# Pairing the state tiles of a selective scan: u*B, the states and h*C in one SBUF tile, on one Trainium2 core

## The chip, the cores and the metric

The kernel runs on one core of a Trainium2 chip. The metric is the device time of one execution in microseconds (us), the median of several runs. The core's engines are named as in the profile: PE (TensorE), DVE (VectorE), ACT (ScalarE), POOL (GpSimd) and SP (SyncE, which issues the DMAs of the main loop). SBUF is the on-chip memory that all of them reach; PSUM is the smaller memory that the matmuls write to.

## The reference

The input is x, 32 x 96 x 56 x 56, in float32. A ConvNeXt block (7x7 depthwise convolution, layer norm, a 96-384-96 GELU network, residual) is followed by two Mamba layers over the 3136 pixels of each image as a sequence, a fusing 1x1 convolution with a pooled branch, a batch norm and a residual. Nearly all of the time goes to the two Mamba layers:

```
xs, z  = split(layernorm(seq) @ in_w)           # 192 channels each
xc     = silu(conv4(xs) + conv_b)
dt, Bm, Cm = split(xc @ xproj_w)                # 6, 16, 16
delta  = softplus(dt @ dt_w + dt_b)
h[t]   = exp(delta[t] * A) * h[t-1] + delta[t] * Bm[t] * xc[t]   # 192 channels x 16 states
y      = sum over states of h * Cm + Dp * xc
seq    = seq + (y * silu(z)) @ out_w
```

With u = delta * xc, the work of the recurrence for each channel and state is: e = exp(delta*A), the product u*B, the scan h = e*h + u*B, the product h*C, and a sum of h*C over the 16 states.

## The kernel before

A sequence of 3136 is cut into 4 chunks of CH = 784 tokens. A **stage** is one chunk of one image in one layer, so there are 32 x 4 x 2 = 256 stages. The 192 channels are six blocks j of 32 channels; with 4 of the 16 states on the partitions beside the 32 channels, one block has NG = 4 groups g. So a stage has 24 **steps** n, one scan of 128 x 784 each. The block's copy of delta (`d4`) and the copies of B and C (`bc`) are spread over the partitions by DMAs from DRAM that SP issues.

The order of each engine's instructions is written out by hand (`manual_schedule`). The final loop goes through the steps; at each it issues the exps of one or two steps ahead (`exps`), the carry of the state (`keep_state`), the scan (`scan`), and the sum over states of three or four steps back (`add_up`). Everything else (projections, norms, the ConvNeXt block and the convolution of later images, DMAs) consists of small pieces, each with a slot number that says after which step of which stage it is issued. Each engine then runs its own list in order and waits on semaphores.

In step (j, g) of the kernel before:

- ACT writes e = exp(A*d4) (L890). For the four blocks j = 0, 1, 3, 4 and g = 0, 1, 2 it goes into an SBUF tile `da`; for g = 3, and for the blocks in `POOLED` (2 and 5), into a PSUM slot `w`.
- u*B: for j = 0, 1, 3, 4, PE spreads u over the partitions into a PSUM slot `u4` (`spread`, L905) and DVE multiplies by B (`times_b`, L878). The product for g = 0, 1, 2 goes to PSUM (`w`, or `u4` in place), and for g = 3 to an SBUF tile `da`. For the `POOLED` blocks POOL multiplies in SBUF (`pooled`, L915, into a `da`).
- DVE scans (L938, TENSOR_TENSOR_SCAN), from e and u*B into slot g of `ring`, a tile of four states called h in the profile. One of the scan's two tensors is always in PSUM and the other in SBUF:

```
e = wide(g % 2)[:, 0:CH] if in_psum(j, g) else product_tile(S, j, g)
db = da if in_psum(j, g) else S.u4[:, 0:CH] if g == 2 else S.w
```

- POOL multiplies h by C into `da` (L942), one instruction of 128x784 for each step.
- PE adds the four states of each channel up with a 0/1 matrix `ssum` (L975), two matmuls of 32 columns for each step. When two blocks are done, DVE multiplies the sum by silu(z) (`gate`, L956).

`keep_state` (L949) copies the last column of h for the next chunk of the image. `product` (L712) is u = delta*xc on POOL, in two instructions.

Of the kernel before, what the change touches and what calls it, by code (L numbers as in the profile page):

```python
# [37 lines left out]
ALU = mybir.AluOpType  # L38
# [23 lines left out]
def convnext_mamba_kernel(  # L62
# [211 lines left out]
    for i in range(2):  # L274
        d = {}
        lg, lb = column(ln_g[i], C, f"lg{i}"), column(ln_b[i], C, f"lb{i}")
        wz = const.tile([C + 1, 2 * DIN], F32, name=f"inw{i}", tag=f"inw{i}")
        norm_weights(wz, in_w[i], lg, lb)
        wx = const.tile([C + 1, 4, DIN], F32, name=f"wx{i}", tag=f"wx{i}")
        nc.gpsimd.dma_start(wx, taps[i].partition_broadcast(C + 1))  # L280
        for k in range(4):
            nc.vector.tensor_tensor(wx[:, k, :], wx[:, k, :], wz[:, 0:DIN], ALU.mult)
        d["wx"], d["wz"] = wx, wz[:, DIN : 2 * DIN]
# [60 lines left out]
    with ExitStack() as main:  # L344
# [7 lines left out]
        def work(shape, name, bufs):  # L352

            pool, n = (pre[0], 3) if pre else (wp, bufs)
            return pool.tile(shape, F32, name=name, tag=name, bufs=n)
# [42 lines left out]
        xins = {}  # L398

        def block0(b, c, s):  # L400
# [16 lines left out]
            def load_x():  # L417
                if s == 0:
                    xins[b, c] = work([C, CH], "xin", 1)
                    nc.sync.dma_start(xins[b, c], x[b, :, c * CH : (c + 1) * CH])  # L420
# [36 lines left out]
            def down():  # L457
                v["ps"] = psum(2)
                nc.tensor.matmul(
                    v["ps"][0:C, 0:HC], eye, xins[b, c][:, tok(s)], start=True, stop=False  # L460
                )
                for f in range(NF):
                    nc.tensor.matmul(
                        v["ps"][0:C, 0:HC], w2_sb[:, f, :], v["gl"][:, f, :],
                        start=False, stop=(f == NF - 1),
                    )

            def residual():
                xs = xins[b, c][:, tok(s)]
                nc.scalar.activation(  # L470
                    xs, v["ps"][0:C, 0:HC], AF.Identity, bias=b2ls,
                    accum_out=batch_sums[b][:, k : k + 1],
                )
                if s == 1:
                    nc.sync.dma_start(x1_d[b][:, c * CH : (c + 1) * CH], xins.pop((b, c)))
# [6 lines left out]
            def pool():  # L482
                ps = psum(2)
# [4 lines left out]
            def fuse():  # L488
                ps = psum(2)
# [9 lines left out]
            last = [(21.5, total), (29.9, pool), (30.9, fuse)] if k == 2 * NCH - 1 else []  # L499
            return last + [  # L500
                (-6, load), (2, load_x), (11.3, center), (12.1, square), (12.4, mean),
                (12.8, root), (14.1, True, norm), (15.6, up), (15.9, gelu), (17.3, down),
                (18.3, residual),
# [28 lines left out]
        PARTS = (0, (NB + 1) // 2), ((NB + 1) // 2, NB)  # L532

        def conv(g, p):
# [11 lines left out]
            def tap(part, dw):  # L546
                first, last = PARTS[part]

                def piece():
                    if dw == 0:  # L550
                        v["ps"] = psum(2)
                    nc.tensor.matmul(  # L552
                        v["ps"][0:R2, 0 : (last - first) * W], v["band"][:, dw, :],
                        xpad[:, first:last, dw : dw + W], start=(dw == 0), stop=(dw == 6),
# [4 lines left out]
            def store(part):  # L559
                first, last = PARTS[part]  # L560
                n = (last - first) * W

                def piece():
                    t = wp.tile([R2, HC], F32, name="sq", tag="sq", bufs=3)
                    nc.scalar.activation(
                        t[:, 0:n], v["ps"][0:R2, 0:n], AF.Identity, bias=cb[:, p : p + 1]
                    )
                    nc.sync.dma_start(
                        conv_d[g][p * R2 : (p + 1) * R2, first * W : last * W], t[:, 0:n]
                    )  # L570

                return piece

            at = (7.7, 8.2, 8.6, 9.2, 9.6, 10.2, 10.4), (18.5, 18.6, 19.2, 20.2, 21.2, 21.3, 22.2)
            return [
                (-1, load), (11.05, store(0)), (22.9, store(1)),
                *[(at[part][dw], tap(part, dw)) for part in range(2) for dw in range(7)],
            ]


        POOLED = (2, 5)
        seqs = {}
# [4 lines left out]
        def prep(S):  # L587
# [77 lines left out]
            def dbl_out():  # L665
# [5 lines left out]
                S.bcs = []  # L671

            def load_bc(gs):
                def piece():
                    for g in gs:
                        t = wp.tile([128, 2, CH], F32, name="bc", tag="bc", bufs=8)
                        for k in range(2):
                            src = v["bd"][NS * k + 4 * g : NS * k + 4 * g + 4, :]
                            nc.sync.dma_start(
                                t[:, k, :], src.unsqueeze(0).broadcast_to([32, 4, CH])  # L680
                            )
                        S.bcs.append(t)

                return piece
# [23 lines left out]
            def product(lo, hi):  # L708
                def piece():
                    if lo == 0:  # L710
                        S.u = wp.tile([128, NQ, HC], F32, name="u", tag="u", bufs=1)
                    nc.gpsimd.tensor_tensor(  # L712
                        S.u[:, lo:hi], v["dl"][:, lo:hi], S.xc[:, lo:hi], ALU.mult
                    )

                return piece
# [21 lines left out]
            def load_d4(j):  # L738
# [10 lines left out]
                (-18, load), (-12.9, center), (-11.9, square), (-11.8, halo), (-11.6, mean),  # L749
                (-11.2, root), (-9, True, norm),  # L750
            ]
            t = (-7.6, -7.5, -6.5, -6, 0, 0.1, 1, 2.3, 3.1, 3.4, 4)
# [7 lines left out]
            elif S is stages[3]:  # L760
# [14 lines left out]
                (max(10.2, t[8] + 1.2), load_bc((0, 1))), (max(13.2, t[8] + 2.2), load_bc((2, 3))),  # L775
                (t[9], dt), (t[10], softplus),
                (max(16.9, t[10] + 1.5), product(0, 2)), (max(18.3, t[10] + 3.1), store_u(0)),
                (25.2, product(2, 3)), (26.3, store_u(1)),
                (max(17, t[10] + 2), load_d4(0)), (max(18, t[10] + 3), load_d4(1)),
                (max(20, t[10] + 3.2), load_u(0)), (23, load_d4(2)),  # L780
                (26, load_d4(3)), (32.9, load_u(1)), (30, load_d4(4)), (35, load_d4(5)),
            ]

        def post(S):
# [54 lines left out]
            pieces = [(7.5, project), (9, move(0)), (10, move(1))]  # L839
            if i == 1:  # L840
                pieces += [(12.9, save), (17.2, stat(0)), (18.2, stat(1))]
# [5 lines left out]
        ring = wp.tile([128, NG, CH], F32, name="h", tag="h", bufs=1)  # L847
        LAG = 3
        LATE = (4, 12)
# [8 lines left out]
        for i, b, c in order:  # L858
            S = Stage()
            S.i, S.b, S.c, S.d, S.da, S.e = i, b, c, lay[i], {}, {}  # L860
# [8 lines left out]
        def in_psum(j, g):  # L869

            return j in POOLED or g == NG - 1

        def product_tile(S, j, g):
            t = S.da[j, g] = wp.tile([128, CH], F32, name="da", tag="da", bufs=11)
            return t

        def times_b(S, out, g):
            nc.vector.tensor_tensor(  # L878
                halves(out), S.u4.rearrange("p (a b) -> p a b", a=2)[:, :, 0:HC],
                halves(S.bcs[g][:, 0, :]), ALU.mult,  # L880
            )

        def exps(n):
# [5 lines left out]
            e = wide(g % 2)[:, 0:CH] if in_psum(j, g) else product_tile(S, j, g)  # L889
# [7 lines left out]
        def spread(n):  # L897

            m, r = divmod(n, NSTEP)
            if m == len(stages) or r // NG in POOLED:  # L900
                return
            S, j = stages[m], r // NG
            S.u4 = wide(0)
            for a in range(2):
                nc.tensor.matmul(  # L905
                    S.u4[:, 512 * a : 512 * a + HC], sel[rows(a), j % 2, :],
# [3 lines left out]
        def pooled(m, j, g):  # L910


            def piece():
                S = stages[m]
                nc.gpsimd.tensor_tensor(  # L915
                    product_tile(S, j, g), S.us[j], S.bcs[g][:, 0, :], ALU.mult
# [4 lines left out]
        def scan(n):  # L921
# [3 lines left out]
            if r in LATE and n >= NSTEP // 3:  # L925
                gate(n - LAG - 2)
            run(n, within)
            if j not in POOLED and g < 2:
                if g == 0:
                    S.w = wide(1)[:, 0:CH]  # L930
                times_b(S, S.w, g)
                if g == 0:
                    times_b(S, product_tile(S, j, NG - 1), NG - 1)
                else:
                    times_b(S, S.u4[:, 0:CH], 2)
            da = S.da[j, g]
            db = da if in_psum(j, g) else S.u4[:, 0:CH] if g == 2 else S.w
            nc.vector.tensor_tensor_scan(  # L938
                ring[:, g, :], S.e.pop((j, g)), db, 0.0 if c == 0 else d["st"][:, j, g : g + 1],
                ALU.mult, ALU.add,  # L940
            )
            nc.gpsimd.tensor_tensor(da, ring[:, g, :], S.bcs[g][:, 1, :], ALU.mult)  # L942

        def keep_state(n):
# [3 lines left out]
            if g % 2 == 1 and S.c < NCH - 1:  # L948
                nc.scalar.copy(  # L949
                    S.d["st"][:, j, g - 1 : g + 1].unsqueeze(2), ring[:, g - 1 : g + 1, CH - 1 : CH]  # L950
                )
# [6 lines left out]
        def add_up(n):  # L958
# [4 lines left out]
            S, j, g = stages[m], r // NG, r % NG  # L963
            q = j // 2
            if j % 2 == 0 and g == 0:
                if j == 4:
                    gate(n - 1)
# [4 lines left out]
            da = S.da.pop((j, g))  # L972
            for a in range(2):
                r0 = 64 * a + 32 * (j % 2)
                nc.tensor.matmul(  # L975
                    S.y[r0 : r0 + 32, 0:HC], ssum, da[:, tok(a)],
                    start=False, stop=(g == NG - 1),
                )
# [159 lines left out]
```

## Time and profile before

| | |
|---|---|
| median of 3 runs | 16962.6 us (16959.04 to 16968.48) |
| the profiled execution | 16951.94 us, span 16950.2 us |
| POOL busy, DVE busy | 15657.7 us, 15667.8 us (92% each) |
| PE busy, ACT busy | 15327.0 us (90%), 11444.5 us (68%) |
| first scan starts, last h*C starts | 560.9 us, 16582.5 us |
| granted TensorE clock | 0.943 of full speed |

Busy time is the time in which an engine had an instruction running. It is counted from an instruction's start to its end, and neighbours on DVE and POOL overlap by some 0.05 us, so a stage is best added up from start to start. About 0.9 ms of the span lies outside the 256 stages: the first convolution and the first image's ConvNeXt block ahead of them, and the batch norm behind them.

### The profile page before, as it was taken

To read this page: it belongs to the slowest core of one execution; us is meant where nothing else is said; L and a number is where in the kernel's file an instruction comes from. 1 tells how busy PE (TensorE), PEld (TensorE's weight loads), DVE (VectorE), ACT (ScalarE), POOL (GpSimd) and SP (SyncE) were. 2 spreads that over 40 slices of the span, in tenths; PEclk is the share of its full clock that TensorE was granted. 3 is DMA by queue.
4 is the path that set the end of the run, shared out by engine and by line. 5 is a ranking of instruction groups with operands and counts; after the bars stand their busy time and mean duration, and the time that the engine had idled before them with its cause. 6 is when DMAs were issued, how large, how long until landed. Compare 5 with 4: busy or idle time off the path is not lost. (4 is left out here: it accounts for less than half of the span.)

```text
span 16950.2 us, 206740 instructions
## 1 busy us (share of the span) xinstructions
PE 15327.0 (90%) x69336; PEld 5507.9 (32%) x69336; DVE 15667.8 (92%) x12351; ACT 11444.5 (68%) x18723; POOL 15657.7 (92%) x8798
## 2 busy tenths in 40 slices
PE   8899999999999999999999999999998888888881
PEld 5333333333333333333333333333332222222220
DVE  8699999999999999999999999999999999999994
ACT  1577777777777777777777777677776777676653
POOL 1699999999999999999999999999999999999991
PEclk9899999999999999999999999999999999999985
DMA  4344444444444444444444444444443433433338
GB/s 113 109 139 142 142 135 140 139 142 141 135 142 140 142 135 140 142 141 137 138 141 141 142 134 141 140 143 137 137 142 131 133 126 129 134 132 133 125 121 280
DMA packets 1303109, 2362.11 MB, mean 139 GB/s; under 512 B 516398, under 2 KB 669242, under 8 KB 1302040
## 3 DMA queue, kind: packets, MB, share of 16 engines
q1 hardware_dynamic: 1292712, 2308.46, 42.0%
q10 hardware_dynamic: 7168, 38.54, 0.6%
q8 instruction: 546, 8.95, 0.2%
q14 instruction: 523, 4.28, 0.1%
q0 software_dynamic: 2160, 1.88, 0.1%
HBM read 1945.97 MB, written 402.41 MB: 139 GB/s over the span
## 5 line engine op out<-in xcount | busy, mean ns | idle before, releaser
L942 POOL TENSOR_TENSOR da<-h,bc 128x784 f32<-128x784 f32 x6144 | 11296.0, 1864 | 428.7 <-DVE h L938 356.3
L975 PE MATMUL y<-da,ssum 128*32 128x392 f32 x24576 | 5193.2, 547 | 232.7 <-POOL da L942 229.1
L890 ACT ACTIVATE w<-d,A 128x784 f32<-128x784 f32 x3072 | 2810.9, 916 | 2442.6 <-DVE h L938 2403.6
L938 DVE TENSOR_TENSOR_SCAN h<-w,st,da 128x784 f32<-128x784 f32 x2304 | 4120.7, 1831 | 267.6 <-ACT w L890 261.5
L938 DVE TENSOR_TENSOR_SCAN h<-da,st,w 128x784 f32<-128x784 f32 x2304 | 4176.3, 1834 | 3.6 <-ACT st L949 3.2
L915 POOL TENSOR_TENSOR da<-us,bc 128x784 f32<-128x784 f32 x2048 | 3811.8, 1861 | 0.0
L878 DVE TENSOR_TENSOR w<-w,bc 128x784 f32<-128x784 f32 x3072 | 2910.6, 978 | 325.6 <-PE w L905 257.4
L890 ACT ACTIVATE da<-d,A 128x784 f32<-128x784 f32 x3072 | 2834.6, 939 | 19.0 <-DMA d<-dd 16.0
L633 PE MATMUL ps<-hn,wx 97*64 97x392 f32 x12288 | 2263.2, 503 | 11.0 <-DVE hn L621 11.0
L975 PEld LDWEIGHTS y<-da,ssum 128*32 128x32 f32 x24576 | 1079.4, 116 | 3366.9 <-issue 2015.7
L905 PE MATMUL w<-u,sel 64*128 64x392 f32 x4096 | 992.4, 560 | 555.8 <-DVE h L938 436.8
L938 DVE TENSOR_TENSOR_SCAN h<-w,da 128x784 f32<-128x784 f32 x768 | 1327.4, 1771 | 125.6 <-ACT w L890 118.0
L938 DVE TENSOR_TENSOR_SCAN h<-da,w 128x784 f32<-128x784 f32 x768 | 1345.4, 1773 | 0.0
L633 PEld LDWEIGHTS ps<-hn,wx 97*64 97x64 f32 x12288 | 797.5, 136 | 1422.4 <-issue 1113.2
L712 POOL TENSOR_TENSOR u<-dl,xc 128x784 f32<-128x784 f32 (+1 forms) x512 | 736.9, 1439 | 471.0 <-ACT dl L698 471.0
L552 PE MATMUL ps<-xpad,band 112*112 112x168 f32 (+1 forms) x5376 | 1086.6, 312 | 0.0
L552 PEld LDWEIGHTS ps<-xpad,band 112*112 112x112 f32 x5376 | 709.8, 175 | 1088.3 <-issue 972.7
L690 PE MATMUL ps<-dbl,dtw 6*64 6x392 f32 x3072 | 728.0, 536 | 310.9 <-ACT dbl L668 310.9
L878 DVE TENSOR_TENSOR da<-w,bc 128x784 f32<-128x784 f32 x1024 | 988.0, 965 | 1.0 <-DMA bc<-bd 1.0
L368 ACT ACT_TABLE_LOAD x759 | 973.8, 1283 | 14.2 <-PEq L1125 0.8
L377 ACT ACTIVATE sq<-ps 96x392 f32<-96x392 f32 x768 | 345.1, 490 | 759.9 <-PE ps L372 343.6
L969 PE MATMUL y<-xc,D 128*128 128x392 f32 x1536 | 790.3, 601 | 32.8 <-DVE z L956 32.8
(152 smaller groups left out, 14579.4 us busy)
## 6 DMA issues: line engine op xcount, KB each, us to landing
bc<-bd SPq DMA_DIRECT2D x2048, 392.0 KB, 6.5
d<-dd SPq DMA_DIRECT2D x1536, 392.0 KB, 3.6
us<-uu SPq DMA_DIRECT2D x512, 392.0 KB, 3.3
dd<-dl SPq DMA_DIRECT2D x512, 294.0 KB, 3.7
band<-band_d SPq DMA_DIRECT2D x192, 343.0 KB, 4.3
uu<-u SPq DMA_DIRECT2D x1024, 49.0 KB, 3.0
cv<-conv_d SPq DMA_DIRECT2D x256, 147.0 KB, 3.4
xin<-in_x SPq DMA_DIRECT2D x128, 294.0 KB, 3.9
```

What stands on the lines that cost most here:

```text
L368: nc.scalar.preload_act_table_set("natural_log_exp_and_others")
L552: nc.tensor.matmul(v["ps"][0:R2, 0 : (last - first) * W], v["band"][:, dw, :], xpad[:, first:last, dw : dw + W], start=(dw == 0), stop=(dw ...
L633: nc.tensor.matmul(v["x", q][rows(a), 0:HC], weights[:, k, 64 * q : 64 * q + 64], v["hn"][:, o : o + HC], start=(k == 0), stop=(k == last),)
L712: nc.gpsimd.tensor_tensor(S.u[:, lo:hi], v["dl"][:, lo:hi], S.xc[:, lo:hi], ALU.mult)
L878: nc.vector.tensor_tensor(halves(out), S.u4.rearrange("p (a b) -> p a b", a=2)[:, :, 0:HC], halves(S.bcs[g][:, 0, :]), ALU.mult,)
L890: nc.scalar.activation(e, S.d4[j], AF.Exp, scale=S.d["A"][:, j, g : g + 1])
L905: nc.tensor.matmul(S.u4[:, 512 * a : 512 * a + HC], sel[rows(a), j % 2, :], S.u[rows(a), j // 2, :], start=True, stop=True,)
L915: nc.gpsimd.tensor_tensor(product_tile(S, j, g), S.us[j], S.bcs[g][:, 0, :], ALU.mult)
L938: nc.vector.tensor_tensor_scan(ring[:, g, :], S.e.pop((j, g)), db, 0.0 if c == 0 else d["st"][:, j, g : g + 1], ALU.mult, ALU.add,)
L942: nc.gpsimd.tensor_tensor(da, ring[:, g, :], S.bcs[g][:, 1, :], ALU.mult)
L969: nc.tensor.matmul(S.y[:, 0:HC], S.d["D"][:, q, :], S.xc[:, q, :], start=True, stop=False)
L975: nc.tensor.matmul(S.y[r0 : r0 + 32, 0:HC], ssum, da[:, tok(a)], start=False, stop=(g == NG - 1),)
```

## The change

The four tensors of a step are laid out anew, and the work is done by pairs (j, h) of two groups:

- One SBUF tile of 128 x 2 x 784, `h`, with 7 buffers, holds u*B of two groups. The scan reads it and writes the states into the same place; h*C is written into it again. The ring of four states and the 11 `da` tiles are gone.
- exps of blocks 0, 1, 3, 4 all go to SBUF, into pair tiles `da` with 2 buffers. Those of the `POOLED` blocks go to PSUM as before. So the scans of the four blocks now have both of their tensors in SBUF.
- `spread` puts u of a block into one of two PSUM slots (j % 3) at steps named in `SPREADS`, and all four products of a block are made by DVE ahead of its first scan (`WS`).
- h*C is one POOL instruction for two groups (128 x 1568), issued after the second scan of a pair, and so are the products of the `POOLED` blocks. In chunks that have a successor the last column is left out (128 x 2 x 783); ACT copies the state and multiplies the two last columns by C itself (`keep_state`).
- B and C have tiles of their own (`bp` with 3 buffers, `cp` with 4), each for two groups.
- The sum over states is issued twice for two blocks: 16 matmuls in which four in a row write the four column tiles of 32 (2 blocks x 2 halves of the chunk).
- u = delta*xc is one POOL instruction; the convolution of later images is 7 matmuls of 280 columns in place of 14 of 168 and 112; x of the ConvNeXt block is loaded and stored by halves of a chunk; `in_w` is kept only where it is needed. Slot numbers and the steps of `gate` and `add_up` change.

The core of the diff:

```diff
-            return j in POOLED or g == NG - 1
+            return j in POOLED
...
+                S.da[j, h] = wp.tile([128, 2, CH], F32, name="da", tag="da", bufs=2)
...
+                S.h[j, h] = wp.tile([128, 2, CH], F32, name="h", tag="h", bufs=7)
...
-        def times_b(S, out, g):
+        def times_b(S, j, g):
             nc.vector.tensor_tensor(
-                halves(out), S.u4.rearrange("p (a b) -> p a b", a=2)[:, :, 0:HC],
-                halves(S.bcs[g][:, 0, :]), ALU.mult,
+                halves(states(S, j, g // 2)[:, g % 2, :]),
+                S.u4[j].rearrange("p (a b) -> p a b", a=2)[:, :, 0:HC],
+                halves(S.bc[0, g // 2][:, g % 2, :]), ALU.mult,
             )
...
-            e = wide(g % 2)[:, 0:CH] if in_psum(j, g) else product_tile(S, j, g)
+            e = wide(g % 2)[:, 0:CH] if in_psum(j, g) else pair(S, j, g // 2)[:, g % 2, :]
...
-            S.u4 = wide(0)
+            u4 = S.u4[j] = wide(j % 3)
...
-                    product_tile(S, j, g), S.us[j], S.bcs[g][:, 0, :], ALU.mult
+                    states(S, j, h), S.us[j].unsqueeze(1).broadcast_to([128, 2, CH]), S.bc[0, h],
+                    ALU.mult,
...
-            da = S.da[j, g]
-            db = da if in_psum(j, g) else S.u4[:, 0:CH] if g == 2 else S.w
+            if j not in POOLED:
+                for k in WS[g]:
+                    times_b(S, j, k)
+            h = states(S, j, g // 2)
             nc.vector.tensor_tensor_scan(
-                ring[:, g, :], S.e.pop((j, g)), db, 0.0 if c == 0 else d["st"][:, j, g : g + 1],
-                ALU.mult, ALU.add,
+                h[:, g % 2, :], S.e.pop((j, g)), h[:, g % 2, :],
+                0.0 if c == 0 else d["st"][:, j, g : g + 1], ALU.mult, ALU.add,
             )
-            nc.gpsimd.tensor_tensor(da, ring[:, g, :], S.bcs[g][:, 1, :], ALU.mult)
+            if g % 2 == 1:
+                S.da.pop((j, g // 2), None)
+                hc = h[:, :, 0 : CH if c == NCH - 1 else CH - 1]
+                nc.gpsimd.tensor_tensor(hc, hc, S.bc[1, g // 2][:, :, 0 : hc.shape[2]], ALU.mult)
...
+                for k in range(2):
+                    nc.scalar.activation(
+                        h[:, k, last], h[:, k, last], AF.Identity,
+                        scale=S.bc[1, g // 2][:, k, last],
+                    )
...
-            da = S.da.pop((j, g))
-            for a in range(2):
-                r0 = 64 * a + 32 * (j % 2)
-                nc.tensor.matmul(
-                    S.y[r0 : r0 + 32, 0:HC], ssum, da[:, tok(a)],
-                    start=False, stop=(g == NG - 1),
-                )
+            hs = [S.h.pop((2 * q + k, half)) for k in range(2)]
+            for g in range(2):
+                for k in range(2):
+                    for a in range(2):
+                        r0 = 64 * a + 32 * k
+                        nc.tensor.matmul(
+                            S.y[r0 : r0 + 32, 0:HC], ssum, hs[k][:, g, tok(a)],
+                            start=False, stop=(half == 1 and g == 1),
+                        )
```

## Prediction

> **What bounds the kernel now.** I read the busy times first, then the 40 slices, then the costliest groups, then the groups by form and the scan's own line, and last the waits of VectorE (DVE) and GpSimd (POOL).
>
> ```profile
> PE 15327.0 (90%) x69336; PEld 5507.9 (32%) x69336; DVE 15667.8 (92%) x12351; ACT 11444.5 (68%) x18723; POOL 15657.7 (92%) x8798
> ...
> DVE  8699999999999999999999999999999999999994
> ACT  1577777777777777777777777677776777676653
> POOL 1699999999999999999999999999999999999991
> ```
>
> DVE and POOL are full in every slice of the 256 stages; there is no stage with another limit. The stages run from the first scan at 560.9 us to the end of the last h*C at 16,584 us: 16,023 us, or **62.6 us for a stage**, with 927 us of the span outside them.
>
> ```profile
> L942 POOL TENSOR_TENSOR da<-h,bc 128x784 f32<-128x784 f32 x6144 | 11296.0, 1864 | 428.7 <-DVE h L938 356.3
> L938 DVE TENSOR_TENSOR_SCAN h<-w,st,da 128x784 f32<-128x784 f32 x2304 | 4120.7, 1831 | 267.6 <-ACT w L890 261.5
> L938 DVE TENSOR_TENSOR_SCAN h<-da,st,w 128x784 f32<-128x784 f32 x2304 | 4176.3, 1834 | 3.6 <-ACT st L949 3.2
> L915 POOL TENSOR_TENSOR da<-us,bc 128x784 f32<-128x784 f32 x2048 | 3811.8, 1861 | 0.0
> L712 POOL TENSOR_TENSOR u<-dl,xc 128x784 f32<-128x784 f32 x256 | 473.8, 1851 | 471.0 <-ACT dl L698 471.0
> L712 POOL TENSOR_TENSOR u<-dl,xc 128x392 f32<-128x392 f32 x256 | 263.2, 1028 | 0.0
> ```
>
> What to see here: POOL has 24 h*C and 8 u*B in each stage; from start to start they stand 1.815 us apart in the timeline (six in 10.94 us), so 32 x 1.815 + 1.80 + 0.98 (u) = 60.9 us, and 428.7/256 = 1.7 us of waiting: the 62.6. DVE in the same way: 24 scans at 1.77 (1.79 with a carried state, 1.72 without) = 42.5, 16 products at 0.88 = 14.1, gates, norms 2.8: **59.4 us**, and 3.2 us of waits, mostly for e in PSUM and for the copies of u. So POOL comes first by little, and DVE is close behind.
>
> Then the inputs. In each scan one tensor is `w` (PSUM) and the other `da` (SBUF). The scan's own line shows how little these vary beside a POOL that is always reading SBUF:
>
> ```profile
> L938 DVE TENSOR_TENSOR_SCAN h<-da,st,w x2304: 1817/1837/1847, 620.7 to 16569.4; 128x784 f32<-128x784 f32 x192
> L938 DVE TENSOR_TENSOR_SCAN h<-w,st,da x2304: 1819/1827/1852, 627.8 to 16578.6; 128x784 f32<-128x784 f32 x192
> ```
>
> Minimum and maximum lie 2% apart (1817 to 1852 ns). The other DVE work of the stages (times_b, gate, the norms) also has a PSUM input. The trace has no DVE instruction with two SBUF tensors beside a POOL instruction that computes.
>
> [...] the two forms of L712 here give (1851 - 1028)/392 = 2.10.
>
> **The change part by part, for one stage.**
>
> 1. Pairs on POOL. With 2.10 ns an element a POOL instruction has 1851 - 784 x 2.10 = 205 ns that don't grow. 1568 elements: 205 + 3293 = 3.50 us, against two of 1.86. u in one piece (1176): 2.67 against 2.88. From start to start (0.05 less each): 16 x 3.45 + 2.62 = **57.8 us in place of 60.9**, 3.1 less, on the path. The u operand read twice and 783 columns for 784 change nothing that I can price: 0, bounds -0.3 and +0.5 us.
>
> 2. The scans of blocks 0, 1, 3, 4: 16 of 24 now read e and u*B from SBUF, while POOL reads SBUF all the time. [...] What excludes each other must be added up: 16 x 3.50 + 2.67 = 58.7 of POOL (whole durations, as a start can no longer hide under a neighbour) and 16 x 1.815 = 29.0 of scans (1.83 carried, 1.77 not, three to one), together 87.7[...]: **89.5 us**. The other 30 us of DVE (8 scans of the pooled blocks with e in PSUM, 16 products, gates, norms) can run beside POOL. Lower bound: starts that hide and no hand-over, 57.8 + 16 x 1.77 = 86.1. Upper bound: [...] POOL's present 1.7 of waits: 93.1. Of these I take 89.5. This is the whole forecast[...].
>
> 3. Who waits: behind a blocked scan, DVE's queue holds the next products and gates; behind a blocked h*C, POOL's holds u*B of the pooled blocks. The seven h tiles let DVE run ahead, so POOL has always a pair waiting [...].
>
> 4. The seventh tile: tiles are used in turn, so the products of block 4 (step 16) take the tile of pair (2, 0), which is free only when POOL has done pair (3, 0), complete at step 13, and PE has summed both. That is 3.45 us and 16 matmul instructions: 3.4 us at the rate of L975 now (5193/24576 = 0.21 each), half of it at best; I take 2.5. DVE has two scans and the norms (1.45) in between, 5.0 us: 1.0 us of DVE wait, bounds 0 and 3. [...]
>
> 5. ACT: 12 pairs get two tiny multiplies in three chunks of four, 18 a stage; nearest row is the state copy (L949, 178 ns): 3.3 us on an ACT with 11444.5/256 = 44.7 of 62.6 us. They stand ahead of exps that are one and two steps early; POOL's pair waits for neither column. 0, bounds 0 and +1 us.
>
> 6. PE: sums in four column tiles at once instead of two, and 7 convolution matmuls in place of 14. L975 has 5193 us busy; at best half of it goes. DVE's waits for y are 110 us in all, so this is worth 0 to 0.4 us a stage; I take 0, as it lies beside POOL and DVE.
>
> 7. DMAs: B and C move the same bytes in as many issues; x by halves adds a load and a store every two stages on SP, the convolution saves a store a stage. DVE and POOL wait for DMAs 1 us in all the stages, with DMAs busy 43%: 0. New slots for norms, projections, stores and loads of u and delta: 0, bounds -1 and +1, covered by the same slack. POOL's queue: `product` at 16.9 now carries the third part that stood at 25.2, priced in item 1.
>
> Sum: 927 + 256 x 89.5 = **23,840 us**; the bounds 86.1 and 93.1 give 22,970 and 24,760. The profiled execution (16,951.9) stands 11 us below the median (16,962.6), nothing against this.
>
> **The rivals.**
>
> *No contention for scans* (0.18 in all). A scan takes twice as long as a product for the same 784 elements (1.77 against 0.88)[...]. For it: [...] this trace has no such pair. [...] Then POOL needs 57.8 us and DVE 59.4 plus waits; I take 1.5 (item 4 and half a microsecond of the present 3.2, as e of the 16 scans and the copies of u stand earlier): 60.9, and 927 + 256 x 60.9 = **16,520 us, faster**. The point that decides is POOL's slack: (62.6 - 57.8)/16 = 0.30 us of blocked POOL for each scan, a sixth of its length. Below that the change wins, above it loses.
>
> [...] A scan then takes from POOL only its own reads, one pass over 784, as long as a product: 0.88 us. 57.8 + 16 x 0.88 = 71.9, or **19,330 us**. [...]
>
> *The seventh tile decides.* With no contention and PE late by 4 us in item 4, the stage is back at 62.6 to 63.1: 16,950 to 17,080 us, no change. PE's full slices speak for it, its relief (item 6) against.
>
> *The change does not do what it says*: the built program's POOL list has 128x1568 and 128x2x783 instructions and its scans read `da` and h, both SBUF tiles, so this is left out.
>
> **How the numbers follow.** Contention for the whole scan 0.78, shared by elements 0.04, none and faster 0.15, none and equal 0.02, none and slower 0.01. Runs of this kernel tell 0.2% (34 us) from no change. So slower 0.83, same 0.02, faster 0.15. The likeliest case gives 23,840. The range begins at 19,000, below the second slow case, and ends at 24,900, over the upper bound: it leaves out the no-contention cases and little else. The likeliest case's own range is 22,900 to 24,900.
>
> **What would show it.** Right: the sixteen scans or the POOL pairs (or gaps ahead of them, put down to nothing in particular) grow by some 27 us a stage, while the eight scans with e in PSUM stay near 1.83 and DVE plus POOL overlap less; an h*C alone takes near 3.5 us. ACT and PE fall to about 50% and 55% of the span. Wrong: scans h<-da,h at 1.8 us back to back beside POOL pairs of 3.5 us, and a span under 17,000 us. A POOL pair far from 3.50 us would fault item 1; DVE waits for PE ahead of the block-4 products, item 4.

## The result, and the profile after

The changed kernel takes **23005.9 us** (median of 4 runs, 23001.52 to 23014.34) against 16960.8 us for the kernel before (median of 4): a ratio of 1.357, 95% interval 1.354 to 1.359. The forecast was 23,840 us, in a range of 19,000 to 24,900. From the first scan (562.4 us) to the end of the last h*C (22,639.6 us) a stage takes 86.2 us in place of 62.6; the forecast's sum had 89.5.

The page of the changed kernel, the part on busy time and the slices of the two engines:

```profile
PE 15675.8 (68%) x66648; PEld 5844.3 (25%) x66648; DVE 21459.4 (93%) x12353; ACT 12517.2 (54%) x23139; POOL 18792.6 (82%) x4446
...
DVE  6999999999999999999999999999999999999995
...
POOL 0888888888888888888888888888888888888882
```

DVE still looks full, though its work is the same. That is the trap of this view: an instruction that is held up counts as busy, as the next lines show. The groups by form show where the busy time was added (line, engine, operation, tiles and shapes, count, busy us, mean ns, idle before):

```profile
L931 POOL TENSOR_TENSOR h<-h,cp 128x1566 f32<-128x1566 f32 x2304 | 10523.0, 4586 | 2299.5 <-DVE h L924 2294.3 <-PE ps L675 5.2
L924 DVE TENSOR_TENSOR_SCAN h<-da,st,h 128x784 f32<-128x784 f32 x3072 | 10008.9, 3296 | 0.4 <-ACT da L881 0.4
L924 DVE TENSOR_TENSOR_SCAN h<-da,h 128x784 f32<-128x784 f32 x1024 | 3214.2, 3177 | 0.0
L924 DVE TENSOR_TENSOR_SCAN h<-w,st,h 128x784 f32<-128x784 f32 x1536 | 2725.0, 1822 | 0.4 <-ACT w L881 0.4
L949 DVE TENSOR_TENSOR z<-y,z 128x392 f32<-128x392 f32 x768 | 416.7, 543 | 798.1 <-PE y L967 798.1
```

The scans that read `da` and `h`, both in SBUF, have a mean of 3.2 to 3.3 us; those that read `w` in PSUM and `h` still have 1.82. The idle time ahead of the slow ones is 0.4 us in all: they were issued and then waited inside. The scan's and h*C's own lines give minimum, median and maximum:

```profile
L924 DVE TENSOR_TENSOR_SCAN h<-da,st,h x3072: 1812/1837/13728, 643.2 to 22623.5; 128x784 f32<-128x784 f32 x192
L924 DVE TENSOR_TENSOR_SCAN h<-w,st,h x1536: 1811/1819/1849, 673.9 to 22634.1; 128x784 f32<-128x784 f32 x192
...
L931 POOL TENSOR_TENSOR h<-h,cp x3072: 3469/3520/10520, 566.0 to 22636.1; 128x1566 f32<-128x1566 f32 x129, 128x1568 f32<-128x1568 f32 x63
```

A scan with two SBUF inputs takes either the usual 1.8 us or up to 13.7; an h*C 3.5 or up to 10.5. With a PSUM input the maximum is 1.85. In the timeline the two engines can be laid side by side (start us, us; several instructions merged). First POOL, then DVE:

```profile
8026.32 18.59 POOL L931 TENSOR_TENSOR h<-h,cp 128x1566 f32<-128x1566 f32 x2 [1.73 <-DVE h L924]
8044.88 3.54 POOL L906 TENSOR_TENSOR h<-us,bp 128x1568 f32<-128x1568 f32 x1
```

```profile
8026.62 1.83 DVE L924 TENSOR_TENSOR_SCAN h<-da,st,h 128x784 f32<-128x784 f32 x1
8028.39 1.00 DVE L605 TENSOR_TENSOR hn<-seq,ps 96x392 f32<-96x392 f32 x2
8029.31 1.83 DVE L924 TENSOR_TENSOR_SCAN h<-da,st,h 128x784 f32<-128x784 f32 x1
8031.07 3.58 DVE L868 TENSOR_TENSOR h<-w,bp 128x784 f32<-128x784 f32 x4
8034.58 7.06 DVE L924 TENSOR_TENSOR_SCAN h<-da,st,h 128x784 f32<-128x784 f32 x4
8041.57 1.82 DVE L924 TENSOR_TENSOR_SCAN h<-w,st,h 128x784 f32<-128x784 f32 x1
```

Two h*C take 18.6 us instead of 7. The times fit progress while DVE does its products (from 8031.07, a PSUM input) and after the last scan with two SBUF inputs (8041.6): 3.5 us each. During the four scans from 8034.58 POOL stands still, and DVE loses nothing (7.06 us for the four). Elsewhere DVE is the loser: one scan took 12.1 us while POOL did three pairs. Again POOL, then DVE:

```profile
8051.04 13.91 POOL L931 TENSOR_TENSOR h<-h,cp 128x1566 f32<-128x1566 f32 x4
8064.92 3.52 POOL L906 TENSOR_TENSOR h<-us,bp 128x1568 f32<-128x1568 f32 x1
```

```profile
8057.99 12.10 DVE L924 TENSOR_TENSOR_SCAN h<-da,h 128x784 f32<-128x784 f32 x1
```

That scan ends at 8070.09, which is 1.65 us after POOL's u*B (8068.44). So does every other held scan: 1634 scans of this trace took over 1.95 us, and each of them ends 1.64 to 1.66 us after the end of a POOL instruction. So none got past its first 0.2 us while POOL was at work (a scan alone takes 1.8). Laid together over all stages (an instruction counted from start to end), h*C, u*B, u and the scans with two SBUF inputs cover 85.6 of the 86.2 us.

### The profile page after: what moved, and what is told of

Its sections match the earlier page's. It is cut to its first block, busy times and chain, and to the rows that moved or that the text cites. A ratio compares the mean times of both kernels' runs of the same rounds, so it can differ in the third digit from the quotient of the medians.

```text
span 23000.6 us, 198556 instructions
## 1 busy us (share of the span) xinstructions
PE 15675.8 (68%) x66648; PEld 5844.3 (25%) x66648; DVE 21459.4 (93%) x12353; ACT 12517.2 (54%) x23139; POOL 18792.6 (82%) x4446
## 4 chain that ended last, share of the span: by engine, by line
DVE 42%; issue 23%; POOL 17%; PE 12%; DMA 4%; ACT 2%; SPq 0%; DVEq 0%; POOLq 0%; ACTq 0%
DVE h L924 36%; POOL h L931 14%; DVE h L868 4%; PE ps L617 3%; PE w L896 3%; PE y L967 3%; POOL h L906 2%; PE ps L176 2%; DVE z L949 1%; POOL u L695 1%; DMA us<-uu 1%; DMA fr<-x_d 1%; PE ps L443 1%; DMA uu<-u 1%; ACT da L881 1%
## 5 line engine op out<-in xcount | busy, mean ns | idle before, releaser
L931 POOL TENSOR_TENSOR h<-h,cp 128x1566 f32<-128x1566 f32 (+1 forms) x3072 | 13523.6, 4417 | 3316.4 <-DVE h L924 3307.1
L924 DVE TENSOR_TENSOR_SCAN h<-da,st,h 128x784 f32<-128x784 f32 x3072 | 10008.9, 3296 | 0.4 <-ACT da L881 0.4
L906 POOL TENSOR_TENSOR h<-us,bp 128x1568 f32<-128x1568 f32 x1024 | 4505.4, 4400 | 34.4 <-DMA us<-uu 20.1
L967 PE MATMUL y<-h,ssum 128*32 128x392 f32 x24576 | 3496.1, 609 | 1438.5 <-POOL h L931 1437.8
L868 DVE TENSOR_TENSOR h<-w,bp 128x784 f32<-128x784 f32 x4096 | 3685.6, 959 | 320.5 <-PE w L896 301.6
L924 DVE TENSOR_TENSOR_SCAN h<-da,h 128x784 f32<-128x784 f32 x1024 | 3214.2, 3177 | 0.0
L924 DVE TENSOR_TENSOR_SCAN h<-w,st,h 128x784 f32<-128x784 f32 x1536 | 2725.0, 1822 | 0.4 <-ACT w L881 0.4
L546 PE MATMUL ps<-xpad,band 112*112 112x280 f32 x2688 | 1227.5, 590 | 950.8 <-ACT dl L683 950.8
L443 PE MATMUL ps<-hz,w_sb 97*128 97x392 f32 x1536 | 1067.6, 867 | 1149.7 <-DVE hn L605 1149.3
L967 PEld LDWEIGHTS y<-h,ssum 128*32 128x32 f32 x24576 | 838.0, 125 | 3787.2 <-POOL h L931 1987.4
L941 ACT ACTIVATE h<-h,cp 128x1 f32<-128x1 f32 x4608 | 1106.0, 287 | 114.0 <-ACT st L939 1.5
```

The lines of the kernel that those rows point to most:

```text
L443: nc.tensor.matmul(v["pss"][f][:, 0:HC], w1_sb[:, f * 128 : (f + 1) * 128], hn0s[s], start=True, stop=True,)
L546: nc.tensor.matmul(v["ps"][0:R2, 0 : NB * W], v["band"][:, dw, :], xpad[:, :, dw : dw + W], start=(dw == 0), stop=(dw == 6),)
L868: nc.vector.tensor_tensor(halves(states(S, j, g // 2)[:, g % 2, :]), S.u4[j].rearrange("p (a b) -> p a b", a=2)[:, :, 0:HC], halves(S.bc[0 ...
L906: nc.gpsimd.tensor_tensor(states(S, j, h), S.us[j].unsqueeze(1).broadcast_to([128, 2, CH]), S.bc[0, h], ALU.mult,)
L924: nc.vector.tensor_tensor_scan(h[:, g % 2, :], S.e.pop((j, g)), h[:, g % 2, :], 0.0 if c == 0 else d["st"][:, j, g : g + 1], ALU.mult, ALU ...
L931: nc.gpsimd.tensor_tensor(hc, hc, S.bc[1, g // 2][:, :, 0 : hc.shape[2]], ALU.mult)
```

## The experiments

The theory to test: **a scan with two SBUF inputs and a POOL instruction that reads SBUF exclude each other**, so that their times add up. The rival: what else the change brought makes the time, that is the long pair instructions, the work in place, the h tiles in turn or ACT's tiny multiplies. What an expectation says ahead of "The rival" is the theory's. Each of the first five kernels below was executed once; executions of one kernel lie at most 0.04 ms apart here, and the differences read from them are ten times that or more.

**Take the second SBUF input away.**

```diff
-                h[:, g % 2, :], S.e.pop((j, g)), h[:, g % 2, :],
+                h[:, g % 2, :], S.e[j, g] if j in POOLED else S.u4[j][:, 0:CH], h[:, g % 2, :],
```

> The changed kernel, but the 16 scans of blocks 0, 1, 3, 4 read their multiplier from the PSUM copy of u in place of e in SBUF (so the exps are still made but not used; a small matmul fills the gap of the copy). [...] with one SBUF input a scan no longer excludes POOL, so all scans fall to 1.76-1.85 us, POOL's pairs to 3.5 us, and the stage is DVE's 59.4 us plus 1 to 2.5 us of waits: 60.5 to 62 us, a span of 16,400 to 16,800 us. The rival (the long pair instructions, the tiles worked in place, or the seven h tiles make DVE wait): nothing of that changes, so it stays near 86 us a stage, 23,000 us.

Measured: 16326.4 us (beside 16943.2 for the kernel before), 60.1 us a stage, a little under the range expected. All else of the change is still there, but the exps are made and not used.

```profile
L935 POOL TENSOR_TENSOR h<-h,cp 128x1566 f32<-128x1566 f32 x2304 | 8061.3, 3525 | 258.0 <-DVE h L928 241.0 <-PE w L900 15.8
```

```profile
L928 DVE TENSOR_TENSOR_SCAN h<-w,st,h x4608: 1814/1844/1929, 619.7 to 15952.7; 128x784 f32<-128x784 f32 x192
```

No scan is over 1.93 us, and POOL's h*C has a mean of 3525 ns. The rival falls: pairs, work in place, tiles and ACT together don't make the kernel slower here. As these scans don't wait for their exps, this is a lower bound for what the rest of the change is worth, not a kernel.

**Give the kernel before a second SBUF input**, in 4 and in 12 of its 24 scans (for 12, with g in (0, 1, 2)):

```diff
             db = da if in_psum(j, g) else S.u4[:, 0:CH] if g == 2 else S.w
+            if j not in POOLED and g in (0,):
+                db = S.bcs[g][:, 0, :]
```

> The kernel before, but in blocks 0, 1, 3, 4 the scan of g = 0 reads the SBUF tile of B in place of u*B in PSUM (the product is still made, not used): 4 of 24 scans with two SBUF inputs, POOL single instructions, no pairs. [...] POOL's 60.9 us plus 4 x 1.77 = 68.0 us a stage, 927 + 256 x 68.0 = 18,340 us (17,700 to 18,700). The rival (pairs or the work in place cost the time): 16,950 us.

> As the run with 4 scans, for g = 0, 1 and 2: 12 of 24 scans of the kernel before with two SBUF inputs. [...] 60.9 + 12 x 1.77 = 82.1 us a stage, 21,950 us (21,300 to 22,700), on a line with 0 and 4 scans. The rival (pairs or the work in place): 16,950 us.

Measured: 18405.7 and 21211.1 us, or 68.3 and 79.2 us a stage (62.6 with none). Without pairs and without work in place the time comes back, by 1.4 us for each such scan. The first agrees with its sum (68.0) in part by luck: the sum leaves out the 1.7 us that POOL waits in the kernel before, and counts 1.77 us for each scan. The second is short of its sum (82.1) and just under its range. The exclusion is there, but in both runs a scan costs less than its 1.77 us. First the new form with 4 scans, then the scan's own line with 12:

```profile
L940 DVE TENSOR_TENSOR_SCAN h<-da,st,bc 128x784 f32<-128x784 f32 x768 | 2647.3, 3447 | 2.2 <-ACT st L951 2.2
```

```profile
L940 DVE TENSOR_TENSOR_SCAN h<-da,st,bc x2304: 1818/3358/7145, 637.9 to 20825.6; 128x784 f32<-128x784 f32 x192
L940 DVE TENSOR_TENSOR_SCAN h<-w,st,da x2304: 1816/1832/1853, 649.9 to 20836.3; 128x784 f32<-128x784 f32 x192
```

Within one kernel and for the same operation on the same line, only the form with two SBUF tensors (da and bc) is stretched.

**Shorter instructions on POOL.**

```diff
-                nc.gpsimd.tensor_tensor(hc, hc, S.bc[1, g // 2][:, :, 0 : hc.shape[2]], ALU.mult)
+                for k in range(2):
+                    nc.gpsimd.tensor_tensor(
+                        hc[:, k], hc[:, k], S.bc[1, g // 2][:, k, 0 : hc.shape[2]], ALU.mult
+                    )
```

and the same for u*B.

> The changed kernel with POOL's h*C and u*B one group at a time (two instructions of 783 or 784 columns in place of one of 1566 or 1568). [...] POOL's own work goes back to 32 x 1.815 + 2.6 = 60.7 us, plus 28.3 of scans: 89.0 us a stage, 23,700 us (23,400 to 24,200), 0.7 ms slower than the change. The rival (a long POOL instruction holds the scans up, so shorter ones leave gaps for DVE): faster than the change's 23,006 us.

Measured: 22579.2 us, 84.6 us a stage: faster than the change by 0.43 ms, where my sum said 0.7 ms slower. The sum was wrong, and the timeline shows how. POOL, then DVE, of this kernel:

```profile
8000.17 9.87 POOL L931 TENSOR_TENSOR h<-h,cp 128x783 f32<-128x783 f32 x3
8010.00 3.33 POOL L908 TENSOR_TENSOR h<-us,bp 128x784 f32<-128x784 f32 x1
```

```profile
8001.77 9.91 DVE L923 TENSOR_TENSOR_SCAN h<-da,st,h 128x784 f32<-128x784 f32 x3
```

In this stretch the engines take turns, and a turn of one h*C and one scan takes 9.87/3 = 3.29 us. From start to start without contention they are 1.815 and 1.77, 3.585 together. So each turn is 0.295 us shorter than the sum, 0.15 for each change of hands. The ends of the scans show where it comes from: each of the 3835 held scans of this trace ends 1.64 to 1.66 us after the end of a POOL instruction, where a scan that is not held takes 1.82 from start to end. So part of a scan passes while POOL is still at work. For POOL the same is worked out, not seen: 784 x 2.10 ns = 1.65 us is the part that grows with the columns, and 1.65 and 1.65 make up the turn. Counted in the order of their ends, the hands change 30.6 times a stage here and 18.4 times in the change; 89.0 - 30.6 x 0.15 = 84.4 us against 84.6 measured, though the 0.15 is from this same trace. The rival's reason (gaps for DVE) does not fit the trace either, as there are no gaps: h*C, u*B, u and these scans cover 84.55 of the 84.58 us.

**POOL writes only.** Each h*C becomes two memsets:

```diff
-                nc.gpsimd.tensor_tensor(hc, hc, S.bc[1, g // 2][:, :, 0 : hc.shape[2]], ALU.mult)
+                for _ in range(2):
+                    nc.gpsimd.memset(hc, 0.0)
```

> The changed kernel with each h*C replaced by two memsets of the same columns on POOL: it writes SBUF and reads none of it (so h*C is left out). If only POOL's reads exclude the scans: left to exclude are 4 u*B and u (4 x 3.5 + 2.6 = 16.6 us a stage) and 28.3 of scans, 45 us, less than DVE's 59.4; scans beside memsets stay at 1.83 and the stage is 60 to 65 us (some scans wait for a u*B), 16,300 to 17,600 us. If any POOL access excludes them: two memsets at some 1.4 us (from 0.75 us for 784 columns) make 12 x 2.8 = 33.6 us more, 78 us a stage, 21,000 us, and memsets or scans are stretched in the trace.

Measured: 18588.0 us, 69.0 us a stage, between the two expectations.

```profile
L932 POOL MEMSET h<- x6144: 1392/1402/1452, 567.2 to 18215.9; 128x1566 f32 x149, 128x1568 f32 x50
```

```profile
L906 POOL TENSOR_TENSOR h<-us,bp 128x1568 f32<-128x1568 f32 x1024 | 5308.8, 5184 | 597.8 <-PE y L968 299.3 <-ACT da L881 85.0 <-ACT st L940 72.2
L868 DVE TENSOR_TENSOR h<-w,bp 128x784 f32<-128x784 f32 x4096 | 3683.3, 960 | 937.5 <-PE w L896 904.5 <-POOL h L906 30.3
```

Of 6144 memsets none was held up (1392 to 1452 ns), though 2699 of them overlap a scan with two SBUF inputs; 3575 of these 4096 scans took their usual 1.8 us. What still collides is u*B, which reads: a mean of 5.18 us for 3.52. Each of the 521 held scans ends 1.65 us after the end of a u*B (or of u), not of a memset. So reading is what excludes here, as expected, and writing by memset doesn't. The time above my 60 to 65 us comes from collisions with u*B (6.0 us a stage added to scans) and from 904.5 us of products that wait for the copy of u (3.5 us a stage); I had let u*B fall beside work that doesn't collide.

**A version without the collision.** The pairs on POOL and the work in place stay. ACT writes e of g = 0, 1, 2 into the pair tile, DVE puts these products into PSUM (`w`, or the copy of u in place) as the kernel before does, and g = 3 the other way round. The `da` tiles go, h has 9 buffers, and three of the four steps in `SPREADS` move by one.

```diff
-        WS = ((0, 1, 2, 3), (), (), ())
+        WS = ((0, 3), (1, 2), (), ())
...
-            return j in POOLED
+            return j in POOLED or g == NG - 1
...
-                h[:, g % 2, :], S.e.pop((j, g)), h[:, g % 2, :],
+                h[:, g % 2, :], S.e.pop((j, g)),
+                h[:, g % 2, :] if in_psum(j, g) else S.u4[j][:, 0:CH] if g == 2 else S.w,
```

> A whole kernel: pairs on POOL, in place, as in the change, but e and u*B placed so that each scan has one PSUM tensor: ACT writes e of g = 0, 1, 2 into the pair tile and DVE puts u*B of these into PSUM; for g = 3 the other way round. The da tiles go, h has 9 buffers. [...] no exclusion, POOL needs 57.8 us and DVE 59.4 plus the waits for the spread of u and for e in PSUM that the kernel before has too (1.0 and 1.5 us a stage), 61.0 to 62.4 us: 16,540 to 16,900 us, faster than before by 0.3 to 2.5%. The rival (the pairing itself makes DVE wait, for tiles or for POOL): no faster than before, 16,950 us or more.

Measured: **16421.4 us** (median of 5), ratio to the kernel before 0.968, interval 0.967 to 0.970: it beats both kernels. Its groups:

```profile
L926 DVE TENSOR_TENSOR_SCAN h<-h,st,w 128x784 f32<-128x784 f32 x2304 | 4195.1, 1835 | 1.0 <-ACT h L881 1.0
L934 POOL TENSOR_TENSOR h<-h,cp 128x1566 f32<-128x1566 f32 x2304 | 8059.0, 3524 | 415.1 <-DVE h L926 413.5 <-POOL h L934 0.3
L926 DVE TENSOR_TENSOR_SCAN h<-w,st,h 128x784 f32<-128x784 f32 x2304 | 4111.3, 1830 | 49.5 <-ACT w L881 48.1 <-issue 0.4
L866 DVE TENSOR_TENSOR w<-w,bp 128x784 f32<-128x784 f32 x3072 | 2912.5, 979 | 193.9 <-PE w L896 75.8 <-DVE h L926 1.4 <-issue 0.4
```

Scans and pairs keep their bare durations, and a stage takes 60.5 us, below my 61.0 to 62.4. Now DVE is the bound: its own 59.4 us leave 1.1 of waits. For the copies of u and for e in PSUM it waits 76 and 150 us in all, where the kernel before had 257 and 380. Those waits were smaller than I had carried over, and the time lies under its range too (16,540 to 16,900 us); why isn't tested.

## Why the prediction was right

The exclusion, its place and its direction were right, and the time was 3.5% below the forecast. No trace had shown the exclusion when the forecast was made: there it was an assumption. The runs show it for the scan: 1.85 us at most in the changed kernel with one SBUF input, up to 13.7 us with two. By its steps:

1. **Pairs.** 3.50 us forecast, 3.52 measured (median of h*C, and the mean without contention); u in one piece 2.67 and 2.69. The 3 us of POOL's work in a stage are saved, but this shows only where no scan with two SBUF inputs is in the way: 16,421 us in the fastest version, 23,006 in the change.
2. **The exclusion.** Forecast 89.5 us a stage, measured 86.2, at the lower bound of 86.1. The mis-sized term is the hand-over: of the 3.4 us between forecast and bound, 1.6 come from taking whole durations and the rest from a price for each hand-over that no trace had shown. The run with single instructions shows the opposite sign, 0.15 us saved for each change of hands. With that the change should stand at 86.1 - 18.4 x 0.15 = 83.3 us. That it stands at the lower bound instead is luck: the saving and a loss of 2.9 us cancel. An estimate from the trace places most of the loss. Let a scan hold POOL out for its last 1.65 us, and a POOL instruction hold scans out for its last 2.10 ns an element (3.29 us for a pair; the 1391 pairs on POOL that took over 3.65 us end 3.27 to 3.38 us after the end of a scan with two SBUF inputs). Then neither holds the other out for 1.4 us a stage at changes of hands (nothing with single instructions) and for 1.7 us between two scans in a row (0.12 for each of the 6.8, or 0.8 us, was allowed for). Why the pairs on POOL leave these gaps unused stays open. In the timeline above, the first h*C gained nothing from the 0.85 us between the scans ending at 8028.5 and beginning at 8029.3, when DVE did two norms with a PSUM input.
3. **Who waits.** Not as written: POOL does not always have a pair waiting, it idles 3307 us in all (12.9 us a stage) for states. But that is while scans with two SBUF inputs are under way: for 85.6 of the 86.2 us one of the two engines has an instruction under way that can exclude the other's, and the sum holds. Nor do the engines take turns as I priced them: four scans or three pairs in a row can keep the other out. What was held waited for the end of an instruction of the other engine (the 1634 scans end 1.64 to 1.66 us after one, the 1391 pairs 3.27 to 3.38 us), but that doesn't say who is next.
4. **The seventh tile.** 1.0 us forecast without contention; in the run with a PSUM multiplier DVE's products wait 33 us in all, 0.1 us a stage. So the rival that rested on it has nothing to show for it.
5. **ACT's tiny multiplies** take 287 ns, not 178: 18 of them make 5.2 us (18 of 178 ns are 3.2, not the 3.3 of the forecast). They are hidden all the same, with ACT at 54%.
6. **PE** did not fall to 55% of the span: 68%. The sums got cheaper (L967 3496 us for 5193, and 2732 in the run with a PSUM multiplier), but the granted clock fell from 0.943 to 0.781 and the other matmuls took longer (the projections of hn and wx 549 ns for 503). DVE waits 798 us for the sums, where it was 110, but the sums themselves wait 1438 us for POOL's h*C. PE is off the path, as priced.
7. **DMAs**: no DVE instruction of the stages waits for one, and POOL waits 20 us for them in all.

The rival without contention said 16,520 us; the version that avoids the second SBUF input has 16,421. Its arithmetic was sound apart from item 4 and the carried-over waits; only its premise was wrong. The sharing element by element (19,330 us) is refuted by the scans and pairs that stand still for whole instructions, and by the held scans, which all need the same 1.65 us after POOL's end.

## What to carry to other kernels

Before a tensor is moved from PSUM to SBUF, count for each VectorE scan that would then read two SBUF tensors how long GpSimd reads SBUF beside it. Here the two times added up (a stage went from 62.6 to 86.2 us), and the busy view hid it, as a held instruction counts as busy (DVE 92% before, 93% after). No other VectorE instruction had two SBUF inputs in the stages, so for others the runs show nothing. The mark of it was a group of one operation whose mean depends on the memory of its inputs, with a minimum at the bare duration and a maximum of several times that. The saving on POOL (205 ns for each instruction left out by the estimate; two h*C of 1.86 us became one of 3.52) was real: with it and the rest of the change the kernel is 3.2% faster, once each scan keeps one input in PSUM. How much of this the pairs alone bring wasn't separated.

## What the runs showed of the hardware that was not expected

- A change of hands between such a scan and a POOL instruction can cost less than nothing against bare start-to-start times: beside single POOL instructions a turn of scan and product of 784 columns takes 3.29 us for 3.585. In the five kernels that have such scans 9960 were held, and every one ends 1.64 to 1.66 us after the end of a POOL instruction that reads, where a scan alone takes 1.75 to 1.85.
- The two engines don't always take turns. Beside single POOL instructions the engines mostly alternate, but 68 of the 4096 scans took 5 to 15 us there, behind several POOL instructions. Beside pairs, four scans in a row passed a waiting h*C (10.5 us), and a scan stood through three pairs (12.1 us). What decides wasn't found.
- The granted TensorE clock was lower in every variant than in the kernel before: 0.943 before, 0.781 in the change, 0.784 with single instructions, 0.839 with memsets, 0.859 and 0.907 with 12 and 4 scans, 0.890 with the PSUM multiplier, 0.867 in the fastest version. PE was busy for a smaller share of the span in the change (68% for 90%) and in the fastest (83%). No run was made on this.
